# A state-space scan in tiles of 4 states x 32 channels, with the other stages run between the scan tiles

## The chip, the cores and the metric

The kernel runs on one core of one Trainium2 chip. The metric is the device time of one execution in microseconds.

## The reference, cut to what matters

The input x is 8 images of 384 channels x 32 x 32 (1024 tokens), f32. A mixer with a selective scan comes first, then a feed-forward net (FFN) with binarised weights and quantised activations.

```python
t = layernorm(x)                              # over channels
xm, z = split(t @ in_proj_w.T)                # 768 inner channels each
xc = silu(causal_conv3(xm) + conv_b)
dt, Bm, Cm = split(xc @ x_proj_w.T)           # 24, 16 and 16 wide
dt = softplus(dt @ dt_proj_w.T + dt_proj_b)
dA  = exp(dt[:, :, None] * A)                 # 768 channels x 16 states
dBu = (dt * xc)[:, :, None] * Bm[:, None, :]
h_t = dA_t * h_{t-1} + dBu_t                  # the scan over 1024 tokens
y_t = sum over the 16 states of h_t * C_t
y = (y + xc * D) * silu(z)
x = x + gelu(y @ out_proj_w.T @ mlp_w1.T + b1) @ mlp_w2.T + b2
x = x + ffn(layernorm(x))                     # not zero in 5 of the 8 images
```

There are 8 x 768 x 16 recurrences of 1024 steps: 768 tiles of 128 partitions x 1024 elements.

## The kernel before

It works in units of 512 tokens. A unit runs its stages one after another. In the scan a tile has one state of 128 channels in each half of its 1024 columns. The state at the end of the first half image is carried over by a small copy on POOL.

```python
for n0 in range(0, NS, NB):                       # NB = 2 states
    bc = stream.tile([P, 2, NB, T], F32, ...)     # rows of B and C on all partitions
    nc.sync.dma_start(bc, rows_cn[:, n0:n0+NB, :].partition_broadcast(P))
    for d in ds_:
        # ... two exps on ACT: da[:, j, :] = exp(a * dt)
        nc.vector.tensor_mul(u, dtx[d]..., bc[:, 0])              # L208
        for j in range(NB):
            nc.vector.tensor_tensor_scan(u[:, j, :], da[:, j, :], u[:, j, :], ...)  # L213
        if half == 0:
            nc.gpsimd.tensor_copy(state[:, d, n0:n0+NB], u[:, :, T-1])
        nc.vector.tensor_mul(u, u, bc[:, 1])                      # L220
        for j in range(NB):
            nc.tensor.matmul(py[d], ident, u[:, j, :], ...)       # L223, sum of the states
```

After the scan come the gate, the output projection and the MLP; after the last unit the FFN. Nothing of another unit is put between scan tiles by the program.

## Time and profile before

| | before |
|---|---|
| time | 6855.95 us, median of 3 (6848.48 to 6856.16) |
| PE, DVE, ACT, POOL busy | 74, 67, 34, 6% |
| moved by DMA | 409 MB |
| packets of the main queue | 18.2% of 16 engines' span |

The next fence is from the page of the kernel before: the busy tenths in 40 equal slices, the main DMA queue (packets, megabytes, share of 16 engines' span), and one row of the DMA issues, whose last column is the median time from issue to landing in us.

```profile
DVE  7759494949586785939494958768593939443333
DMA  2121121212211212112121212121221211200000
q1 hardware_dynamic: 151008, 403.22, 18.2%
...
bc<-rows SPq DMA_DIRECT2D x256, 1024.0 KB, 5.3
```

DVE swings between 9 tenths in the scans and 3 to 5 elsewhere. The DMA engines are busy for 1 or 2 tenths of the time, and a replicated load of 1 MB (bc: two rows each of B and C on all 128 partitions) lands in 5.3 us.

### The profile page before, as it was taken

To read this page: it belongs to the slowest core of one execution; us is meant where nothing else is said; L and a number is where in the kernel's file an instruction comes from. 1 tells how busy PE (TensorE), PEld (TensorE's weight loads), DVE (VectorE), ACT (ScalarE), POOL (GpSimd) and SP (SyncE) were. 2 spreads that over 40 slices of the span, in tenths; PEclk is the share of its full clock that TensorE was granted. 3 is DMA by queue.
4 is the path that set the end of the run, shared out by engine and by line. 5 is a ranking of instruction groups with operands and counts; after the bars stand their busy time and mean duration, and the time that the engine had idled before them with its cause. 6 is when DMAs were issued, how large, how long until landed. Compare 5 with 4: busy or idle time off the path is not lost.

```text
span 6854.0 us, 29767 instructions
## 1 busy us (share of the span) xinstructions
PE 5053.7 (74%) x9244; PEld 1863.5 (27%) x9244; DVE 4579.1 (67%) x4456; ACT 2298.2 (34%) x3124; POOL 431.3 (6%) x544
## 2 busy tenths in 40 slices
PE   6676868686767768686867676776868686778888
PEld 2222313232222222132323222222323232233333
DVE  7759494949586785939494958768593939443333
ACT  4333333324242433333242424343333324122222
POOL 1100020001100110002000110011000200000000
PEclk7888878797878878887878887888878787889999
DMA  2121121212211212112121212121221211200000
GB/s 95 60 66 66 62 78 50 78 49 75 65 62 59 69 58 69 67 58 76 56 72 55 73 57 67 61 66 61 67 72 56 71 58 62 84 12 19 19 19 19
DMA packets 155154, 408.99 MB, mean 60 GB/s; under 512 B 14044, under 2 KB 65500, under 8 KB 154996
## 3 DMA queue, kind: packets, MB, share of 16 engines
q1 hardware_dynamic: 151008, 403.22, 18.2%
q10 hardware_dynamic: 3988, 3.87, 0.2%
q8 instruction: 73, 1.20, 0.1%
q14 instruction: 85, 0.70, 0.0%
HBM read 385.55 MB, written 21.50 MB: 59 GB/s over the span
## 4 chain that ended last, share of the span: by engine, by line
DVE 40%; PE 36%; issue 12%; ACT 6%; POOL 6%; DMA 0%; DVEq 0%; ACTq 0%; POOLq 0%; SPq 0%
DVE u L213 26%; PE pom L266 8%; PE p_h L260 7%; DVE u L208 6%; POOL state L219 5%; PE p_in L105 5%; PE p_y L409 5%; PE p_y L387 4%; PE p_out L240 3%; DVE u L220 2%; PE p_var L128 1%; DVE rstd L131 1%; PE pyd L223 1%; PE p_dbc L162 1%; PE p_var L370 1%
## 5 line engine op out<-in xcount | busy, mean ns | idle before, releaser
L223 PE MATMUL pyd<-u,ident 128*128 128x512 f32 x3072 | 2111.0, 827 | 1298.9 <-DVE u L220 1298.9
L205 ACT ACTIVATE da<-dtd,a_neg 128x512 f32<-128x512 f32 x1536 | 1017.3, 713 | 1886.9 <-DVE u L213 1871.2
L223 PEld LDWEIGHTS pyd<-u,ident 128*128 128x128 f32 x3072 | 668.5, 240 | 2743.9 <-DVE u L220 2203.7
L220 DVE TENSOR_TENSOR u<-u,bc 128x1024 f32<-128x1024 f32 x768 | 936.9, 1220 | 29.4 <-POOL state L219 2.2
L213 DVE TENSOR_TENSOR_SCAN u<-da,state,u 128x512 f32<-128x512 f32 x768 | 942.8, 1266 | 0.0
L208 DVE TENSOR_TENSOR u<-dtxd,bc 128x1024 f32<-128x1024 f32 x768 | 920.9, 1201 | 0.6
L213 DVE TENSOR_TENSOR_SCAN u<-da,u 128x512 f32<-128x512 f32 x768 | 897.3, 1208 | 0.0
L270 DVE SCALAR_TENSOR_TENSOR res<-pom,v_mlp_b,res 128x512 f32<-128x512 f32 x48 | 36.0, 750 | 1204.3 <-PE pom L266 1200.8
L105 PE MATMUL p_in<-t,in_w 128*128 128x512 f32 x1152 | 606.7, 685 | 176.3 <-ACT t L134 108.8
L266 PE MATMUL pom<-g,w 128*128 128x512 f32 x1152 | 539.7, 607 | 0.8 <-ACT g L264 0.8
L260 PE MATMUL p_h<-t,w 128*128 128x512 f32 x1152 | 523.1, 592 | 0.0
L219 POOL COPY state<-u 128x2 f32<-128x2 f32 x384 | 398.5, 1038 | 1645.0 <-DVE u L213 1645.0
L264 ACT ACTIVATE g<-p_h,v_mlp_b 128x512 f32<-128x512 f32 x192 | 131.9, 687 | 832.1 <-PE p_h L260 832.1
L105 PEld LDWEIGHTS p_in<-t,in_w 128*128 128x128 f32 x1152 | 246.3, 220 | 546.5 <-issue 284.6
L409 PE MATMUL p_y<-y,w_W 128*128 128x512 f32 x720 | 325.2, 615 | 39.1 <-ACT y L400 39.1
L387 PE MATMUL p_y<-tn,w_W 128*128 128x512 f32 x720 | 319.1, 605 | 16.9 <-DVE tn L376 16.9
L266 PEld LDWEIGHTS pom<-g,w 128*128 128x128 f32 x1152 | 205.7, 189 | 328.1 <-issue 199.0
L260 PEld LDWEIGHTS p_h<-t,w 128*128 128x128 f32 x1152 | 218.9, 190 | 275.5 <-issue 273.6
L240 PE MATMUL p_out<-xcm,out_w 128*128 128x512 f32 x576 | 263.4, 610 | 3.4 <-ACT z L233 3.4
L392 DVE TENSOR_REDUCE mx<-y 128x1 f32<-128x1024 f32 x60 | 73.1, 1219 | 242.4 <-ACT y L391 242.4
L176 PE MATMUL p_dt<-dbc,dt_w 24*128 24x512 f32 x192 | 138.2, 821 | 104.4 <-ACT e L183 70.0
L233 ACT ACT_TABLE_LOAD x96 | 123.2, 1283 | 241.8 <-DVE xcm L234 240.4
(89 smaller groups left out, 2867.9 us busy)
## 6 DMA issues: line engine op xcount, KB each, us to landing
bc<-rows SPq DMA_DIRECT2D x256, 1024.0 KB, 5.3
w<-in_mlp_w SPq DMA_DIRECT2D x384, 192.0 KB, 2.3
t<-in_x SPq DMA_DIRECT2D x16, 768.0 KB, 4.4
res<-in_x SPq DMA_DIRECT2D x16, 768.0 KB, 4.5
x_mid<-res SPq DMA_DIRECT2D x10, 768.0 KB, 3.8
x<-x_mid SPq DMA_DIRECT2D x5, 1536.0 KB, 7.8
out<-y SPq DMA_DIRECT2D x15, 512.0 KB, 2.7
out<-res SPq DMA_DIRECT2D x6, 768.0 KB, 3.8
```

The source lines that it names most:

```text
L105: nc.tensor.matmul(pm, in_w[:, k, m * P : (m + 1) * P], t[:, k, :], start=(k == 0), stop=(k == KC - 1),)
L205: nc.scalar.activation(da[:, j, :], dt[d], AF.Exp, scale=a_neg[:, d, n : n + 1])
L208: nc.vector.tensor_mul(u, dtx[d].unsqueeze(1).to_broadcast([P, NB, T]), bc[:, 0])
L213: nc.vector.tensor_tensor_scan(u[:, j, :], da[:, j, :], u[:, j, :], 0.0 if half == 0 else state[:, d, n : n + 1], ALU.mult, ALU.add,)
L219: nc.gpsimd.tensor_copy(state[:, d, n0 : n0 + NB], u[:, :, T - 1])
L220: nc.vector.tensor_mul(u, u, bc[:, 1])
L223: nc.tensor.matmul(py[d], ident, u[:, j, :], start=(n == 0), stop=(n == NS - 1))
L240: nc.tensor.matmul(pm, out_w[:, k, m * P : (m + 1) * P], xc[k], start=(k == 0), stop=(k == KD - 1),)
L260: nc.tensor.matmul(ph, w1[:, k, :], t2[:, k, :], start=(k == 0), stop=(k == KC - 1))
L266: nc.tensor.matmul(po[m], w2[:, m * P : (m + 1) * P], g, start=(h == 0), stop=(h == KH - 1))
L387: nc.tensor.matmul(pm, w1[:, k, m * P : (m + 1) * P], tn[:, k, cols], start=(k == 0), stop=(k == KC - 1),)
L409: nc.tensor.matmul(pm, w2[:, k, m * P : (m + 1) * P], y1[:, k, cols], start=(k == 0), stop=(k == KH - 1),)
```

## The change

The intent is that scan work on DVE and matmul work on PE go on at once, and that a scan step costs DVE less.

- A scan tile now holds 4 states x 32 channels over all 1024 tokens. Its exp and its scan are in PSUM; the product u moves to POOL. The tile needs dt and dt * x of 32 channels, each four times on the partitions. They are written to DRAM and read back replicated: each 32 x 1024 block lands on all 128 partitions, in 512 KB.
- Softplus becomes one ACT function, and the gate by z and dt * x move to POOL.
- The sum over the states is a matmul with a 128 x 32 selector, one per 32-channel group, for 4 states at once.
- Everything else (first stage of the next image, last stage of the previous one, FFN) is a generator ("job"), advanced between scan tiles by a table of costs.

The core of the diff, with cuts at "...":

```diff
+SQ = 4
+DQ = P // SQ
...
+        def quad_rows(first, q):
+            r = self.bc.tile([P, L], F32, ...)
+            src = rows[first + q * SQ : first + (q + 1) * SQ, :]
+            nc.sync.dma_start(r, src.unsqueeze(1).to_broadcast([SQ, DQ, L]))
+        def rep(d, j, name):
+            r = self.sc.tile([P, L], F32, tag=name, name=name, bufs=3)
+            src = d[j * DQ : (j + 1) * DQ, :]
+            nc.sync.dma_start(r, src.unsqueeze(0).to_broadcast([SQ, DQ, L]))
...
+                        da = self.ps_da.tile([P, L], F32, tag="da", name="da")
+                        nc.scalar.activation(da, dts[i], AF.Exp, scale=self.a_neg[...])
+                        nc.gpsimd.tensor_mul(u, dtxs[i], b_q[q])
+                        nc.vector.tensor_tensor_scan(da, da, u, 0.0, ALU.mult, ALU.add)
+                        nc.vector.tensor_mul(hc, da, c_q[q])
...
+                    nc.tensor.matmul(
+                        py[jj * DQ : (jj + 1) * DQ, cols], self.fold, hc[:, cols],
+                        start=(q == 0), stop=(q == NQUAD - 1),
+                    )
...
+    COST = {"s1": 146, "s3": 216, "prepare": 30, "f1": 84, "f2": 73}
...
+            for k, _ in enumerate(self.s2(b)):
+                while done < target * (k + 1) / (tiles - 4):
+                    n = step(jobs)
```

Partition p of a tile is state p // 32 and channel p % 32.

## The prediction

> **What bounds the kernel now.** I read the page's engine totals first, then the busy slices and the chain that ended last, then cut one 512-token unit into stages, then looked at single steps of the scan.
>
> ```profile
> PE 5053.7 (74%) x9244; PEld 1863.5 (27%) x9244; DVE 4579.1 (67%) x4456; ACT 2298.2 (34%) x3124; POOL 431.3 (6%) x544
> DVE 40%; PE 36%; issue 12%; ACT 6%; POOL 6%; DMA 0%; DVEq 0%; ACTq 0%; POOLq 0%; SPq 0%
> ```
>
> No engine is full over the span, and the chain is shared by DVE and PE. That means the two take turns. The table of stretches for the second unit (start to scan, scan, output projection and MLP) shows the turns:
>
> ```profile
> core 0: us, PE busy (x) PEld busy (x) DVE busy (x) ACT busy (x) POOL busy (x), PEclk, DMA share, GB/s
> 382.00:447.00 65.00, 48.56 (x93) 17.77 (x91) 34.92 (x43) 34.30 (x46) 1.49 (x6) 0.84 0.21 64
> 447.00:678.50 231.50, 144.19 (x221) 46.86 (x222) 231.40 (x214) 85.06 (x119) 0.00 (x0) 0.79 0.20 67
> 678.50:755.00 76.50, 76.50 (x174) 31.86 (x173) 1.55 (x3) 11.96 (x18) 0.00 (x0) 1.00 0.21 59
> ```
>
> DVE is busy for 231.40 of the scan's 231.50 us; PE for all 76.50 us of the MLP, with DVE at 1.55; 65 us go to a mixed stage of dependent steps. One unit is 373 us, sixteen are 5968, and the FFN that follows has 878 (it starts at 5976 of 6854).
>
> ```profile
> 98.89 2.33 DVE L213 TENSOR_TENSOR_SCAN u<-da,u 128x512 f32<-128x512 f32 x2
> 101.14 1.20 DVE L208 TENSOR_TENSOR u<-dtxd,bc 128x1024 f32<-128x1024 f32 x1
> 101.29 1.10 POOL L219 COPY state<-u 128x2 f32<-128x2 f32 x1 [3.57 <-DVE u L213]
> 102.42 1.23 DVE L220 TENSOR_TENSOR u<-u,bc 128x1024 f32<-128x1024 f32 x1
> 103.56 2.33 DVE L213 TENSOR_TENSOR_SCAN u<-da,u 128x512 f32<-128x512 f32 x2
> ```
>
> This is the timeline inside a scan: one step of 128 x 1024 elements takes 103.56 - 98.89 = 4.67 us, all of it DVE: two scans, the product u, the product with C. There are 768 such steps: 3590 us, over half the span.
>
> ```profile
> L223 PE MATMUL pyd<-u,ident 128*128 128x512 f32 x3072 | 2111.0, 827 | 1298.9 <-DVE u L220 1298.9
> L260 PE MATMUL p_h<-t,w 128*128 128x512 f32 x1152 | 523.1, 592 | 0.0
> 320.29 5.31 PE L260 MATMUL p_h<-t,w 128*128 128x512 f32 x12
> 325.44 5.31 PE L266 MATMUL pom<-g,w 128*128 128x512 f32 x12
> ```
>
> The state sums last 827 ns each because PE starves and runs slow in the scan; the dense MLP starts 12 instructions every 325.44 - 320.29 = 5.15 us, so 0.429 us per instruction is PE's true rate. (A logical f32 matmul shows as two instructions: 0.858 us.)
>
> **What the Trainium skill says.** (1) "SBUF — State Buffer", section Who interferes with whom: a DVE instruction with two SBUF inputs contends with GpSimd reads, one with at most one SBUF input does not. The trace agrees with the first half: the 128x2 POOL copy above lasts 1.10 us and ends with the DVE product L208, while a like copy (L149) outside the scan has a mean of 277 ns. This is why the change puts the scan's data into PSUM. (2) "GPSIMD Engine Reference", section 3.1: f32 tensor_tensor takes about 2.6 cycles per element at 1.2 GHz, 4497 ns for 2048. No run shows one yet; my estimate from that page is 2.3 us for 1024. (3) "TensorE: Matmul & The Clock Gate", Part 3: outputs of 32 columns in distinct column groups run concurrently, three of them 2.38 times as fast. No matmul of the kernel before does this, and the page says nothing of f32. (4) "ScalarE: Activation LUTs", What ACT_TABLE_LOAD costs: about 1283 ns; the trace has 1283.
>
> **The change, part by part.**
>
> *Scan step, DVE.* The tile is again 128 x 1024 and their number again 8 images x 24 x 4 = 768. u moves to POOL: minus 1.20 us. One scan of 1024 replaces two of 512; I take 2.3 us (two in a row take 2.33, one fixed part is saved, PSUM may give it back). The product with C stays at 1.2; reading PSUM need not cost more, as L228 with a PSUM input has 735 ns and L153 from SBUF 750. New step 3.5 us; 768 x 3.5 = 2690 us instead of 3590.
>
> *Other DVE work.* Softplus' five vector operations go to ACT as one function (L186, L187, L189, L190, L192: 39 + 64 + 66 + 66 + 65 = 300 us gone), the gate by z to POOL (66 gone). What stays, from the groups: convolution 190, mixer norms 110, FFN norms 68, gate by D about 60, residual 36, maxima of y1 and y2 about 105, quantisation about 105, weights about 40: 710. Convolution and the SBUF-only scalings now collide with POOL's u products: about 100 by estimate. DVE total 2690 + 710 + 100 = 3500 us.
>
> *PE.* The matmuls are the same: per image 108 (norms, projections, dt) + 180 (output, MLP), five times 84 + 72 for the FFN, so 3084 logical, 6168 instructions x 0.429 = 2650 us. State sums: 768 tiles x 2 = 1536 logical again, 3072 instructions, 1320 us if they follow each other. They alternate between two column groups; as each is two dependent halves I expect at best about 5 slots for 8: 820 us. PE total 3960 without concurrency, 3470 with it.
>
> *POOL.* 768 x 2.3 = 1770, dt times x 96 x 1.2, gate 48 x 2.3: about 2000 us. It has 3.5 us for each 2.3 us product.
>
> *ACT.* One exp of 1024: two of 512 take 1.33 us now (one pair in the scan), so about 1.05; 800 us in all. The rest about 900, table loads between exp and the other functions perhaps 200 x 1.28 = 260. About 2000 us: not a bound, but a late exp stops the scan.
>
> *DMA.* Each dt and dt-x block is read four times over, and dt, dt-x, xc, z, gated y and y1 go through DRAM, weights are streamed: I count 76 MB per image and 25 per FFN image, 740 MB against 409. The SP queue's 403.22 MB took 18.2% of 16 engines' span, that is 323 GB/s while moving, so 740 MB need 2.3 ms.
>
> *Ends.* The first image's whole first stage comes before the first scan tile: 28 us to the first projection as in the trace, 108 x 0.858 = 93 us of PE, some 30 for softplus and the way through DRAM: 150 us. The last image's last stage has nothing beside it: 180 x 0.858 = 154, with load and store 170. The FFN's 878 us go between scan tiles; by the job costs in the program only that last stage is left at the end.
>
> **Sum.** DVE route: 3500 + 150 + 170 = 3820. PE route: it also works in the ends, so 3960 + 50 = 4010, or 3520 with concurrency. On top come stalls. An operation of ACT over 3072 elements is about 2.76 us by estimate (1482 ns for the 1536 of L125 plus 0.83 per element), plus two table loads 5.3; two PSUM buffers for da give exp a slack of only about 2 us beside DVE's 3.5 us step, so about 3 us of DVE per event, some 12 events per image: 300 us. PE waits in the norms (7 and 5 us today) and for its two PSUM buffers. So 3820 + 300 = 4120 if sums run concurrently, 4010 + 350 = 4360 if not. I hold both about equally likely: 4240.
>
> **Rivals.** (A) PE becomes the bound, the sums one after another: for it, 3960 us of dense matmuls and no sign yet of concurrency in f32; then 4.3 to 4.5 ms with PE above 88% busy. (B) DVE stays the bound: its share would be above 80% and the time 3.9 to 4.2 ms. (C) POOL: if its product, pushed by DVE's two-input operations or simply slower than the page says, took over 4.5 us, POOL would set the pace: 768 x 4.5 + 230 + 320 for the ends = 4.0 ms, at 5.5 us 4.8 ms. Against it: the scan and the C product each have only one SBUF input. (D) The queue: all loads and stores are issued by SP in order, about 1600 of them; a load that waits for its buffer holds back the weights behind it. Against it: 740 MB at 323 GB/s fill 55% of 4.2 ms, and the waits of the kernel before hardly name DMA. For it: 3 buffers for loads used in pairs and one for xc and z. It would give 4.6 to 5.2 ms. (E) Overlap fails wholly: DVE 3500 + job matmuls 2650 = 6150 us, still 10% below 6856. That is why I see slower as very unlikely.
>
> **Range and chances.** The floor is about 3820, so low is 3900. (A) with stalls and a mild (D) reach 4750. A tail of perhaps 8% lies above, and little of it reaches 6719 (2% below now). Faster 0.97, within 2% 0.015, slower 0.015.
>
> **What would show it.** Right: scan groups of 1024 at about 2.3 us and products at 1.2; POOL products at 2.3; PE instructions other than sums at a mean near 0.6, granted clock above 0.95; DVE and PE both over 75% busy in all slices but the first and last one or two. The sums' concurrency: the starts of the 8 instructions of a group span about 2.1 us if they share, 3.4 if not. Wrong: a scan from PSUM at 2.6 us or more (+230 us), POOL products over 3.5 us, or waits whose releaser is DMA in the hundreds of us.

## The result, and the profile after

The changed kernel is correct and takes 5475.07 us (median of 4 runs, 5469.40 to 5477.80) against 6856.06 us for the kernel before in the same rounds. The ratio is 0.7983 (95% interval 0.7972 to 0.7995). Ratios here are the mean time of one kernel's fast runs over that of the other's of the same rounds, so not quite the ratio of the medians quoted. It is faster, as predicted, but 725 us above the top of the range and 1235 us above the number.

First the page of the changed kernel: engine totals (busy us, share, instructions), slices, the count of DMA packets, the main queue, the chain.

```profile
PE 3987.9 (73%) x9252; PEld 1397.9 (26%) x9252; DVE 3383.6 (62%) x2345; ACT 1919.2 (35%) x1921; POOL 2112.1 (39%) x1072
...
PE   8574478756878758878387884887758777658859
...
DVE  2598766774575554775646665466664667547860
...
DMA packets 314545, 745.49 MB, mean 136 GB/s; under 512 B 23804, under 2 KB 92924, under 8 KB 314388
...
q1 hardware_dynamic: 311984, 743.26, 41.5%
...
PE 21%; DMA 15%; DVE 7%; issue 4%; POOL 3%; ACT 2%; SPq 0%; POOLq 0%; DVEq 0%; ACTq 0%
```

The turns are gone: the slices no longer swing between 9 and 3. But neither engine is full; after the first slices DVE stands mostly at 4 to 7 tenths. DMA, with 0% of the chain before, now has 15%. (The chain could be followed only over 52% of the span; its shares are used for their order.)

The costliest groups show that the parts of the scan step cost about what was expected (columns: out<-in, shape, count, then busy us and mean ns, then idle time before and its main releaser):

```profile
L313 POOL TENSOR_TENSOR u<-dtx_r,bc 128x1024 f32<-128x1024 f32 x768 | 1836.4, 2404 | 2665.5 <-DVE da L314 2211.3
L314 DVE TENSOR_TENSOR_SCAN da<-da,u 128x1024 f32<-128x1024 f32 x768 | 1733.7, 2286 | 684.4 <-ACT da L309 597.0
L278 PE MATMUL py<-hc,fold 128*32 128x512 f32 x3072 | 1047.1, 721 | 744.7 <-DVE hc L316 704.8
...
L316 DVE TENSOR_TENSOR hc<-da,bc 128x1024 f32<-128x1024 f32 x768 | 910.9, 1213 | 631.5 <-PE py L278 604.3
```

The time is in the idle columns: DVE waits 684 us before the scans and 632 us before the products. The table of stretches, cut at the first and the last scan tile, places it:

```profile
0.00:179.00 179.00, 135.37 (x246) 51.91 (x246) 46.71 (x53) 68.86 (x79) 20.31 (x38) 0.82 0.47 159
179.00:5294.00 5115.00, 3692.54 (x8640) 1276.61 (x8640) 3329.88 (x2285) 1818.36 (x1807) 2089.45 (x1034) 0.83 0.42 137
5294.00:5473.00 179.00, 160.04 (x366) 69.41 (x366) 6.98 (x8) 32.01 (x35) 2.34 (x1) 0.95 0.28 88
```

(After the length come PE, PEld, DVE, ACT and POOL busy, then granted clock, DMA share, GB/s.) The two ends, 358 us, are near the predicted 320. In the middle DVE works 3330 of 5115 us: 1785 us of gaps, where the prediction had put 300 to 350 of stalls. Who ends them stands in the table of waits (us in all, times, longest):

```profile
ACT da L309 <- DMA dt_r<-dt_d: 615.6, 68, 23.5
DVE hc L316 <- PE py L278: 604.3, 110, 24.4
DVE da L314 <- ACT da L309: 597.0, 114, 16.9
...
POOL u L313 <- DMA dtx_r<-dtx_d: 355.5, 60, 25.4
```

Much of DVE's wait for ACT is ACT's wait for the load dt_r, one step later (e1 tests this). One such place, in DVE's timeline:

```profile
2643.59 4.48 DVE L314 TENSOR_TENSOR_SCAN da<-da,u 128x1024 f32<-128x1024 f32 x2
2647.98 2.33 DVE L316 TENSOR_TENSOR hc<-da,bc 128x1024 f32<-128x1024 f32 x2
2650.44 2.30 DVE L314 TENSOR_TENSOR_SCAN da<-da,u 128x1024 f32<-128x1024 f32 x1
2662.07 2.30 DVE L314 TENSOR_TENSOR_SCAN da<-da,u 128x1024 f32<-128x1024 f32 x1 [9.32 <-ACT da L309]
```

and the same moment in the chain (start us, us, what):

```profile
2643.50 0.79 ACT da L309
2644.29 16.47 DMA dt_r<-dt_d
...
2660.85 1.13 ACT da L309
...
2682.23 23.96 DMA dt_r<-dt_d
```

Two tiles take 2650.44 - 2643.59 = 6.85 us when nothing is late, 3.4 a tile, as predicted. Then a load of 512 KB stands in the chain for 16.5 us, soon after another for 24. In the kernel before, twice the bytes landed in 5.3 us.

Two further things were worked out from the DMA records of the traces. From issue to landing dt_r takes 8.5 us at least, 17.4 at the median and 29.5 at most; dtx_r and bc have medians of 12.5 and 17.8. And exactly four packets are in flight in 35.4% of the time; in the kernel before it is 0.5%. The transfers seem to run on four engines. The Trainium skill has the reason: "DMA: Bandwidth & Descriptors", section Why a DMA increments its semaphore by 16 and not by 1, says that the number of engines is the largest one up to 16 that divides the slowest dimension (other than 1) of both sides. Here that dimension is 4 for the source `[SQ, DQ, L]` and 128 for the tile, so 4 engines; in the bc load of before it was 128, so 16. The mean share of 41.5% over 16 engines hides this.

### The profile page after: what moved, and what is told of

It is laid out like the page before. It is cut to its first block, busy times and chain, and to the rows that moved or that the text cites. A ratio compares the mean times of both kernels' runs of the same rounds, so it can differ in the third digit from the quotient of the medians.

```text
span 5473.1 us, 29744 instructions
## 1 busy us (share of the span) xinstructions
PE 3987.9 (73%) x9252; PEld 1397.9 (26%) x9252; DVE 3383.6 (62%) x2345; ACT 1919.2 (35%) x1921; POOL 2112.1 (39%) x1072
## 2 busy tenths in 40 slices
DMA packets 314545, 745.49 MB, mean 136 GB/s; under 512 B 23804, under 2 KB 92924, under 8 KB 314388
## 3 DMA queue, kind: packets, MB, share of 16 engines
q1 hardware_dynamic: 311984, 743.26, 41.5%
q10 hardware_dynamic: 2404, 0.33, 0.0%
## 4 chain that ended last, share of the span: by engine, by line
PE 21%; DMA 15%; DVE 7%; issue 4%; POOL 3%; ACT 2%; SPq 0%; POOLq 0%; DVEq 0%; ACTq 0%
DMA dt_r<-dt_d 6%; PE p_h L143 5%; PE p_o L367 3%; DVE da L314 3%; PE py L278 3%; PE p_out L342 3%; PE p_y L489 2%; PE p_y L143 2%; POOL u L313 2%; DVE hc L316 2%; DMA w<-in_mlp_w 2%; PE p_z L143 1%; DMA y_d<-y 1%; DMA yg_d<-xr 1%; ACT da L309 1%
## 5 line engine op out<-in xcount | busy, mean ns | idle before, releaser
L313 POOL TENSOR_TENSOR u<-dtx_r,bc 128x1024 f32<-128x1024 f32 x768 | 1836.4, 2404 | 2665.5 <-DVE da L314 2211.3
L314 DVE TENSOR_TENSOR_SCAN da<-da,u 128x1024 f32<-128x1024 f32 x768 | 1733.7, 2286 | 684.4 <-ACT da L309 597.0
L278 PE MATMUL py<-hc,fold 128*32 128x512 f32 x3072 | 1047.1, 721 | 744.7 <-DVE hc L316 704.8
L309 ACT ACTIVATE da<-dt_r,a_neg 128x1024 f32<-128x1024 f32 x768 | 853.8, 1116 | 1949.5 <-DVE hc L316 1318.5
L316 DVE TENSOR_TENSOR hc<-da,bc 128x1024 f32<-128x1024 f32 x768 | 910.9, 1213 | 631.5 <-PE py L278 604.3
L367 PE MATMUL p_o<-g,w 128*128 128x512 f32 x1152 | 519.1, 606 | 17.2 <-DMA w<-in_mlp_w 16.2
L143 PE MATMUL p_in<-t,w 128*128 128x512 f32 x576 | 318.9, 711 | 196.7 <-DMA w<-in_in_proj_w 89.0
L143 PE MATMUL p_y<-tn,w 128*128 128x512 f32 x720 | 344.5, 638 | 95.7 <-ACT y L459 72.3
L489 PE MATMUL p_y<-gf,w 128*128 128x512 f32 x720 | 341.1, 633 | 37.2 <-DMA w<-bin_W 29.3
L143 PE MATMUL p_z<-t,w 128*128 128x512 f32 x576 | 276.0, 631 | 40.6 <-ACT xm L199 15.4
```

The lines of the kernel that those rows point to most:

```text
L143: self.nc.tensor.matmul(pm, w[:, k, :], t[:, k, :], start=(k == 0), stop=(k == KC - 1))
L278: nc.tensor.matmul(py[jj * DQ : (jj + 1) * DQ, cols], self.fold, hc[:, cols], start=(q == 0), stop=(q == NQUAD - 1),)
L309: nc.scalar.activation(da, dts[i], AF.Exp, scale=self.a_neg[:, col : col + 1])
L313: nc.gpsimd.tensor_mul(u, dtxs[i], b_q[q])
L314: nc.vector.tensor_tensor_scan(da, da, u, 0.0, ALU.mult, ALU.add)
L316: nc.vector.tensor_mul(hc, da, c_q[q])
```

## The experiments

All start from the changed kernel ("after"). In the quoted expectations theory A is the above, loads on four engines. Its rivals are that the loads are late for their order or their few buffers (B); that PE's sums free the buffers of hc late (C); and that the job table makes the jobs too dense, so PE gets behind in most tiles and has nothing to do in the last ones (D). P and V are defined where they are used.

### e1_sixteen: the same loads in an order that divides by 16

The partitions of a tile are reordered to p = 4 * channel + state. The slowest dimension of the source is then 32. The selector and the layout of A follow. On every engine the instructions and their order are the same as in "after", and so are the bytes.

```diff
-            nc.sync.dma_start(r, src.unsqueeze(0).to_broadcast([SQ, DQ, L]))
+            nc.sync.dma_start(r, src.unsqueeze(1).to_broadcast([DQ, SQ, L]))
...
-            nc.sync.dma_start(r, src.unsqueeze(1).to_broadcast([SQ, DQ, L]))
+            nc.sync.dma_start(r, src.unsqueeze(0).to_broadcast([DQ, SQ, L]))
...
-    a["A_log"] = al.transpose(3, 1, 0, 2).reshape(P, NJ * NQUAD)
+    a["A_log"] = al.transpose(1, 3, 0, 2).reshape(P, NJ * NQUAD)
```

> The four-fold replicated loads (dt_r, dtx_r, bc) now have 32 rows, not 4 copies, as the slowest dimension of their source; number of loads, bytes and the order of the instructions on every engine are unchanged. Theory A (the source's outer 4 puts each replicated load on only 4 of the 16 DMA engines, so it takes 8 to 20 us and everything behind it in the queue waits): loads land in 3 to 6 us, never exactly 4 transfers in flight for a third of the time, ACT's wait for dt_r (616 us) and POOL's for dtx_r (356 us) fall below 100 us each, and the time falls by 400 to 900 us, to 4600 to 5100 us. Theory B (the fixed order on PE, ACT and SP couples the jobs and the scan, the loads are only late because they are issued late): below 2% change, 5370 us or more. Result right.

Measured: correct, 4749.73 us (4747.42 to 4752.54), ratio 0.6928 (0.6916 to 0.6939). The page and the table of waits of e1:

```profile
PE 3885.1 (82%) x9252; PEld 1363.7 (29%) x9252; DVE 3377.3 (71%) x2345; ACT 1921.2 (40%) x1921; POOL 2118.6 (45%) x1072
...
DMA packets 319921, 745.51 MB, mean 157 GB/s; under 512 B 29180, under 2 KB 98300, under 8 KB 319764
...
dt_r<-dt_d SPq DMA_DIRECT2D x192, 512.0 KB, 5.4
dtx_r<-dtx_d SPq DMA_DIRECT2D x192, 512.0 KB, 4.0
```

```profile
DVE hc L316 <- PE py L278: 552.4, 118, 24.3
PE py L278 <- DVE hc L316: 542.5, 165, 16.4
...
DVE da L314 <- ACT da L309: 121.3, 61, 6.2
```

dt_r lands in 5.4 us instead of 17.4, and DVE's wait for ACT falls from 597 to 121 us. Theory A is right: the layout alone is worth 725 us, more than half of the miss. The order in which DRAM is read changed too, but a packet of 4096 bytes takes 160 ns at the median in "after" and 159 in e1 (from the DMA records), so single packets did not get faster. The packets confirm the number of engines. There are 29180 - 23804 = 5376 more packets under 512 bytes, and 192 + 192 + 64 = 448 replicated loads with 12 more engines make 448 x 12 = 5376. Each engine of a load leaves one such packet of 4 bytes.

### e2_split4: the old layout, each replicated load as four loads of 32 partitions

```diff
+            for k in range(SQ):
+                nc.sync.dma_start(r[k * DQ : (k + 1) * DQ, :], src)
```

> The layout of the change is kept, but each replicated load is issued as four loads of 32 partitions, each of which can use all DMA engines; 1344 more issues on the SP queue, some 0.32 us each (430 us of SP). Theory A: about the same gain as with the other layout, 4600 to 5150 us. If the SP queue's issue time is what limits, it is slower than the other layout by over 100 us and perhaps no faster than 5475. The scheduler orders the instructions anew here, so a few per cent either way may come from that. Result right.

Measured: correct, 5097.39 us (5096.43 to 5103.11), ratio 0.7436 (0.7425 to 0.7447). It gains about half of e1's. Its page counts 50684 packets under 512 bytes, and 29180 + 448 x 48 = 50684, so all four parts of each load did use 16 engines. But it issues 1344 more loads, and the order of the program differs from that of "after". The parts land fast (3.3 us at the median on the page), yet POOL waits 481.5 us for dtx_r: by the records of the issues the four parts of one such load are issued over 5.2 us at the median and over 18 us in the slowest tenth. So they are late by their issue. Whether the number of loads or the new order costs the other 348 us was not separated.

### e3_scan_alone_4 and e4_scan_alone_16: only the scan, with four and with sixteen engines

All jobs are left out (wrong results), so that the loads meet neither weights nor PE's other work. Both ran once.

```diff
-        later = deque([("prepare",)])
-        ...
+        for b in range(B):
+            self.st[b] = first[:5]
+            for _ in self.s2(b):
+                pass
```

> Wrong result on purpose: the first stage of image 0, then the 8 x 96 scan tiles with their sums and gates over image 0's data, no jobs beside them, x copied to the result. Layout of the change (4 engines per replicated load). If scan tiles alone run at DVE's 3.5 us: 150 + 768 x 3.5 = 2840 us plus about 20. Theory A: four loads of 5 us in a burst for eight tiles (28 us), with the second of each pair fetched only when its buffer is freed some 1.5 tiles ahead, stall the scan by 5 to 12 us per 8 tiles: 3300 to 4000 us. Theory B: 2850 to 2950 us, all of the loss comes from the jobs.

> Wrong result on purpose: the same scan alone, with replicated loads that can use all 16 DMA engines. Both theories: 2850 to 2950 us; under theory A 300 us or more below the run with 4 engines.

Measured: 3312.23 and 2976.29 us (the second is 26 us above its expected range). The DVE slices of e3 and then of e4:

```profile
DVE  2238989699977899689996999779997799969998
```

```profile
DVE  2269999999999999999999999999999999999998
```

Even alone the scan on four engines has holes; on sixteen DVE is at 9 tenths from the fourth slice on. By itself the layout costs 336 us here, against 725 in the whole kernel, where weights and stores pass the same queue (in "after" the weight load of the MLP took 17.4 us from issue to landing in its slowest tenth, worked out from the records; in e1 its page median is 2.4 to 3.4).

### e5_hc7: e1 with 7 buffers for hc instead of 4

```diff
-                        hc = self.sc.tile([P, L], F32, tag="hc", name="hc", bufs=4)
+                        hc = self.sc.tile([P, L], F32, tag="hc", name="hc", bufs=7)
```

> Built on the 16-engine kernel (4750 us): 7 buffers for hc instead of 4, nothing else in the program (the scheduler may order anew). Theory C: what is left comes from the short queue between DVE and PE: DVE stands 552 us before the C product until PE has done the state sums that free an hc buffer, while PE stands 542 us waiting for hc. Three more tiles (10 us) of slack then bring 150 to 350 us: 4400 to 4600 us, with DVE's wait for py below 250 us. Theory D (in the stretches with jobs PE has simply more work per tile than DVE, so a longer queue only moves the wait): under 2%, 4655 to 4850 us.

Measured: correct, 4670.66 us (4669.38 to 4674.55), ratio 0.6812. It gains 79 us (1.7%), less than theory C expected and within what theory D did: DVE's wait for PE's sums shrinks from 552 to 367 us but does not go. That more buffers only bridge short delays of PE, and do not help while PE has too much to do, is theory D's account; e6 tests it.

### e6_costs: e1 with the job table mended; e7_hc7_costs: both

```diff
-    COST = {"s1": 146, "s3": 216, "prepare": 30, "f1": 84, "f2": 73}
+    COST = {"s1": 110, "s3": 180, "prepare": 30, "f1": 84, "f2": 73}
```

The table was to say how many units of matmul work each job yields. For s1 and s3 it says about 36 too many, so, by replaying the program's loop with its table, the jobs were done after 72 to 81 of an image's 96 tiles, and PE had only sums in the rest.

> Built on the 16-engine kernel: the job costs of s1 and s3 set to the matmuls they yield (110 and 180 instead of 146 and 216), so that the jobs spread over all 92 tiles of an image and not over the first 75. Theory D: PE's work per tile in the stretches with jobs falls from 5.64 x 0.858 + 0.86 = 5.7 us to 4.86 x 0.858 + 0.86 = 5.0 us, and no tiles are left without jobs at the end of an image: 100 to 300 us less, 4450 to 4650. Theory C: under 2%, 4655 to 4850.

> Both: 7 hc buffers and the job costs corrected, on the 16-engine kernel. If C and D both hold, the gains add to some extent: 4250 to 4500 us. If neither holds, 4655 to 4850.

Measured: e6 4508.32 us (4504.54 to 4514.74), ratio 0.6576 (0.6566 to 0.6585), that is 241 us below e1; e7 4495.49 us (4494.59 to 4498.87), ratio 0.6557 (0.6547 to 0.6567). Both are correct. Theory D is right. With the jobs spread evenly the buffers are worth only 13 us more, so most of what they had gained before was the same loss. The totals of e7:

```profile
PE 3807.4 (85%) x9252; PEld 1355.5 (30%) x9252; DVE 3366.7 (75%) x2345; ACT 1932.7 (43%) x1937; POOL 2146.9 (48%) x1072
```

### e8_no_alternation: e1 with the sums of one tile issued together

The prediction argued from sums that alternate between two groups of 32 columns. This run exchanges the two loops, so that the sums of one group follow each other.

```diff
-            for cols in HALVES:
-                for jj, hc in zip(pair, hcs):
+            for jj, hc in zip(pair, hcs):
+                for cols in HALVES:
```

> Built on the 16-engine kernel: the state sums of one 32-column group follow each other (both halves of one tile, then of the other) instead of alternating between two column groups. If the alternation lets two matmuls run at a time (8 instructions start to end in about 1.9 us, as the trace has it), this costs about 1.3 us per group of 8 in PE, 384 groups, 500 us of PE work; with PE busy 82% now, 150 to 500 us of time: 4900 to 5250. If they never ran two at a time, under 2%.

Measured: correct, 4774.67 us (4760.83 to 4780.13), ratio 0.6960: 25 us above e1, where over 150 were expected if the alternation let two sums run at a time. By its time this is the other alternative, "they never ran two at a time". But the start times of the single records say that they do, in both orders. In e1, 133 of the 152 groups of exactly eight sum instructions start as four pairs: 7 ns within a pair, 0.43 us from pair to pair. In e8 it is 131 of 143 groups, with 13 ns within a pair. A group takes about 1.9 us in both. None of the 128-column sums of e10 starts within 40 ns of another.

The program's order tells which two go together. Four instructions of one column group that stand alone between other matmuls never pair (61 groups in e8). Four of one group followed by four of the other do. So sums of different column groups run two at a time, and in e8 a sum of the second group starts 13 ns after the first group's first, ahead of the three between them. That is why the alternation is hardly needed. In e8 28% of the sums start that close to the one before, in e1 40%: e8 loses pairs where other work parts the two groups.

### e9_costs_four_engines: only the job table mended, loads still on four engines

The diff is that of e6, on "after".

> The changed kernel with only the weights of the jobs mended (s1 110, s3 180), its replicated loads still on four DMA engines. If the loads and the density of the jobs are two separate losses, mending the density gives about what it gave with the fast loads, some 240 us: 5200 to 5280 us. If the slow loads are what the scan waits for in any case, the jobs' density hardly matters: above 5400 us. If a thinner stream of jobs also takes the weight loads out of the slow engines' way, the gain is larger: below 5150 us. I expect 5250.

Measured: correct, 5341.26 us (5336.98 to 5352.85), ratio 0.7793. It gains 134 us instead of 241, between the two alternatives. ACT's wait for dt_r is still there, 641.6 us. So each loss hides a part of the other: with the table mended the layout is worth 5341 - 4508 = 833 us, and without it 725.

### e10_wide_sums: e7 with sums over 128 columns

```diff
-                        py[jj * DQ : (jj + 1) * DQ, cols], self.fold, hc[:, cols],
-                        start=(q == 0), stop=(q == NQUAD - 1),
+                        py[:, cols], self.wide[:, jj * P : (jj + 1) * P], hc[:, cols],
+                        start=(q == 0 and jj == 0), stop=(q == NQUAD - 1 and jj == SQ - 1),
```

> The best version so far (sixteen engines, hc in 7 buffers, mended weights: 4495 us) with the sums of the states done over 128 columns again (a zero-padded selector), right results. The 32-column sums take about 0.24 us of TensorE for each recorded instruction (a group of eight starts to its end in 1.91 us); if 128-column ones take twice that, TensorE has some 730 us more to do. Theory P (TensorE is what bounds this version): 5050 to 5250 us. Theory V (VectorE and its coupling to the others bound it): below 4750 us. I expect 5100.

Measured: correct, 4705.72 us (4694.34 to 4718.12), ratio 0.6864. PE's timeline and its group of sums, first of e7, then of e10:

```profile
2016.14 3.62 PE L278 MATMUL py<-hc,fold 128*32 128x512 f32 x16
...
L278 PE MATMUL py<-hc,fold 128*32 128x512 f32 x3072 | 913.4, 656 | 302.0 <-DVE hc L316 287.8
```

```profile
2017.83 10.46 PE L284 MATMUL py<-hc,wide 128*128 128x512 f32 x24
...
L284 PE MATMUL py<-hc,wide 128*128 128x512 f32 x3072 | 1472.3, 624 | 256.9 <-DVE hc L322 157.5
```

One 32-column instruction takes 3.62 / 16 = 0.226 us, one of 128 columns 10.46 / 24 = 0.436. The narrow sums cost 0.52 of the wide ones, as two at a time would have it. In the whole kernel PE's busy time rises by 405 us (3807.4 to 4212.9): the sums take 1472.3 - 913.4 = 559 us more, but the other matmuls 153 less, at a granted clock of 0.953 instead of 0.915. The time rises by only 210, where 5100 us in all were expected. That is the result of Theory V by its number, but e11 shows that V isn't the whole of it.

### e11_few_sums: e7 with a quarter of the sums

```diff
-                    late.append(lambda ...: sums(py, pair, q, hcs))
+                    if q == 0:
+                        late.append(lambda ...: sums(py, pair, q, hcs))
```

> The same best version with only the sums of the first quarter of the states (wrong results on purpose): three quarters of 733 us, 550 us, are taken from TensorE and nothing from the other engines. Theory P: 3950 to 4150 us. Theory V: above 4300 us. In between, both count. I expect 4200, since VectorE alone has 3370 us besides a start of 163 and an end of 180 without scans.

Measured: 4259.51 us (4258.34 to 4265.58), ratio 0.6215; results wrong (the sums of three quarters of the states are missing). 570 us of PE's busy time are gone (3807.4 to 3237.3) and 236 us of the time. The prediction of P (3950 to 4150) fails, V's just fails too: it is the alternative between, both count. One microsecond of PE's busy time is worth 236 / 570 = 0.41 and, by e10, 210 / 405 = 0.52 us. But the other matmuls change against the sums: here the sums take 913.4 - 234.1 = 679 us less and the others 109 more, at a clock of 0.867. For each microsecond of the sums alone it is 0.35 here and 0.38 in e10.

### e12_costs_later: e7 with each pair's sums issued one tile later

```diff
-                        if i == 0:
+                        if i == 1:
                             for f in late:
```

> The same best version with the sums of a pair of tiles issued one tile later, so that TensorE finds their hc ready when it comes to them (PE py waited 288 us and its weight loads 372 us for DVE hc). If TensorE's in-order wait for hc costs the path, 4400 us or less; if those waits lie beside other limits, 4480 to 4510; if hc's buffers come free later and VectorE waits for them, above 4520. I expect 4440.

Measured: correct, 4478.07 us (4473.27 to 4479.92), ratio 0.6531 (0.6521 to 0.6540). It gains 17 us: PE's wait for hc did not shrink (285 us against 288), so the change did not remove the delay that it was meant for, and where the 17 us come from isn't shown. This is the fastest version found, 997 us below the changed kernel.

## Why the prediction was right or wrong

**Direction and mechanism: right.** The stages now overlap, and the time fell by 20%. The sign given for a full overlap failed, though: DVE and PE over 75% busy in nearly all slices; they stand at 62 and 73% over the span.

**Scan step: right.** Scans of 1024 out of PSUM take 2286 ns (2.3 predicted) and products 1213 (1.2); two tiles take 6.85 us where nothing is late, 3.4 a tile for 3.5.

**DVE total: right, and so were the collisions.** 3383.6 us for 3500. The convolution's scaling (L205) has a mean of 1983 ns where a POOL product runs beside it (43 times) and 540 where none does (53); the same comparison over all such DVE operations gives about 90 us by estimate, for 100. The scans, with one SBUF input, keep between 2233 and 2299 ns in all 768 records, so the second half of the prediction's point (1) agrees too. The page excepts its 2-port modes from that, which the prediction leaves out; L205, with one tensor as input, did collide.

**POOL and ACT: right.** Products of 2404 ns (2.3 us), total 2112 for 2000; ACT 1919 for 2000, exps 1116 ns for about 1050. Rival C is out.

**PE: the sums do share, the clock was missed.** The starts of a group of eight span 1.32 us at the median, below the 2.1 set for "they share" (3.4 if not): two at a time, so 4 slots for 8 where 5 were hoped for. Point (3) of the prediction thus holds in f32; only the alternation is hardly needed for it (e8). PE's 3988 us look like the 3960 without concurrency by accident: busy time includes starved instructions. The granted clock, expected above 0.95, was 0.838, and 0.882 in e1. Over the runs here it rises with PE's busy share: 0.597 at 47% (e3), 0.838 at 73%, 0.953 at 90% (e10).

**Ends: right.** 179 + 179 = 358 us for 320.

**DMA: the step that failed.** "The SP queue's 403.22 MB took 18.2% of 16 engines' span, that is 323 GB/s while moving, so 740 MB need 2.3 ms." The bytes were right (743), and so was the busy time: 41.5% of 5473 us is 2271 us. What was wrong is the silent premise that any transfer uses all 16 engines. The 448 replicated loads used four. A packet of 4096 bytes takes 160 ns by the records (median; the mean is 193), so a 512 KB load of 128 packets takes at least 128 x 0.160 / 4 = 5.1 us for 1.3 on sixteen. All of them keep four engines busy for 448 x 5.1 = 2290 us. With that median, by estimate, and the rest (2271 x 16 - 448 x 128 x 0.160 = 27160 us of engine time) spread over 16, those four are busy for 2290 + 1700 = 3990 us, 73% of the span, and the other twelve for 31%. The weights, spread over all engines, have to pass those four too. So the slow loads came late for exp, exp for the scan, the scan for the sums: 1785 us of gaps on DVE in the middle for the 300 to 350 predicted. That premise also dismissed rival (D), "740 MB at 323 GB/s fill 55% of 4.2 ms": its direction, late loads, came true (its range of 4.6 to 5.2 ms did not), but through the engines of a load and not through the order in the queue. With sixteen engines and the same order ACT waits 33.9 us for dt_r instead of 615.6. The prediction's own alarm, "waits whose releaser is DMA in the hundreds of us", is what showed it.

**The program's job table: a second step that failed.** "The FFN's 878 us go between scan tiles; by the job costs in the program only that last stage is left at the end" is true of the end, but it took the table's costs on trust. Its own count of the matmuls of an image, 108 and 180, stood beside the table's 146 (s1) and 216 (s3), but nothing compared the two. That cost 241 us (e6 against e1), or 134 (e9 against "after").

**The stalls: mis-sized.** With both mended (e6, 4508 us) the time lies inside the predicted range, but 268 us remain above 4240, with the larger buffers 255. Since the sums do share, the branch that applies is the prediction's 4120, so it is 375 with the larger buffers. In e7's middle stretch DVE works 3312 and PE 3520 of 4151 us:

```profile
163.00:4314.00 4151.00, 3519.78 (x8649) 1236.88 (x8647) 3312.17 (x2285) 1832.33 (x1824) 2123.91 (x1032) 0.92 0.49 169
```

So DVE still stands still for 839 us where that branch had 300: 539 more, the ends 22 more, DVE's work 188 less than the 3500, together the 373 by which e7's span of 4493 us exceeds 4120. The prediction had taken the work of one route and added small stalls. e10 and e11 show that neither route alone is the bound. My reading, argued and not shown: two engines that are 80 and 85% busy, coupled by two da buffers and in-order queues, wait for each other at different times. The table of waits of e7 names no single one: DVE waits 245 us for PE's sums, 191 for the MLP's last matmuls (p_o), 118 for exp and 106 for POOL's u. What holds most of the 839 us stays open; more hc buffers (13 us) and later sums (17 us) are not it.

| step | us | from |
|---|---|---|
| the changed kernel | 5475 | |
| replicated loads on 16 engines | -725 | e1 |
| job table mended | -241 | e6 |
| 7 hc buffers | -13 | e7 |
| sums one tile later | -17 | e12 |
| best version | 4478 | |

## What to carry to other kernels

Before spreading a transfer's bytes over all DMA engines in an estimate, look at the slowest dimension of both of its sides: a replicated load that begins with a dimension of 4 runs on 4 engines, and exchanging two dimensions gives 16 for nothing else. A mean DMA share over 16 engines does not show this; the count of small packets for each load and the time from issue to landing do. When work is interleaved by a hand-made table of costs, check the table against what the jobs yield, and when two engines are both near 80% busy, count on a part of each microsecond saved on one of them: here between a third and a half.

## What the Trainium skill lacked or had wrong

- "DMA: Bandwidth & Descriptors" has the rule for the number of engines, down to the leading broadcast of few copies as its example (section Rules for kernel authors), and it held: 4 for a source of 4 x 32 x 1024 and 16 for 32 x 4 x 1024 (5376 more completion packets for 448 loads). What it lacks is the time that this costs: 512 KB landed in 17.4 us at the median instead of 5.4, and the kernel took 15% more time (5475 against 4750 us).
- "TensorE: Matmul & The Clock Gate", Part 3, gives the gain of 32-column outputs in distinct column groups and says nothing of f32. Here f32 sums in two column groups ran two at a time: the two of a pair start 7 ns apart, and an instruction took 0.226 us against 0.436 with 128 columns. It also says that matmuls start strictly in the program's order. In e8, where four instructions of one group come before four of the other, 131 of 143 groups of eight ran as four pairs all the same: one of the second four starts 13 ns after the first, ahead of the rest of the first four.
